# Edge-gated graph layer: the gates' turn ahead of the hot tiles' products, and those products in alternation with the segment sums

## The chip, the cores and the metric

The kernel runs on one core of a Trainium2 chip. A core has five engines with a queue each: PE (matrix products), DVE (vector work), ACT (activations and scaled copies), POOL (here only the issue of indirect gathers) and SP (DMA issue). SBUF holds the working data and PSUM takes what PE writes. The metric is the device time of one execution in microseconds (us), lower is better; the median of several runs counts.

## The reference: what is computed

A graph of 12,500 nodes with 128 features each and 412,500 directed edges, sorted by destination, self loops among them. For each edge the difference of two rows is taken, a gate is computed from it, and the gated differences are summed per destination. The result is added to the input and normalised row by row.

```python
theta = x[dst] - x[src]
w = jax.nn.sigmoid(jax.nn.relu(theta @ W1 + b1) @ W2 + b2)
agg = jax.ops.segment_sum(w * theta, dst, num_segments=n_nodes)
indeg = jax.ops.segment_sum(jnp.ones((dst.shape[0], 1), x.dtype), dst, num_segments=n_nodes)
out = layernorm(x + agg + indeg * (x @ W4 + b4))      # eps 1e-5, no scale or shift
```

All is float32; in this input b1 is scaled by 26.638.

## The kernel before

**Parts.** The edges are worked off in parts. After 18 parts of another kind (`early_part`) come 246 "hot" parts, `part(s)` with s from 18 to 263, and four calls that drain what is open. Two parts make a block of 104 destinations (`WB`); s is even for the first half of a block and odd for the second, which the code keeps as `h`. A hot part is a software pipeline: it turns and gates the hot edges of part t = s + 1, weighs the gathered edges of part s, and brings sums of part s − 1 or s to the block's accumulator `pa`.

**Two kinds of edges.** The sources that are used most are held in SBUF as tables of rows (`tabs`). Edges with such a source, the hot edges, get their rows as a matrix product on PE: a 0/1 tile (`of`, made by DVE) times a table. `hot_products` (L1064 to L1083) issues 24 such bf16 products a part, in four groups of six; three groups go to the PSUM tile `pd`, the fourth to spare columns (from 3P on) of the tile `px`, which the program calls `halves[1]`. `hot_out` copies `pd` into `xT` in SBUF (L1096, ACT), `last_out` copies the spare columns of `px`, by the same line. The other edges are gathered: POOL issues eight indirect DMAs for each part (L405, `gather(s + 3)` from `spread_ahead`), into `zbuf`. The first of the eight carries a wait, `paced[s + 3] = newest[0]`: `newest[0]` is the latest product or sum that the program has issued on PE, so the gathers of a set wait for the end of PE's work in part s − 1.

**One part on PE.** In this order: `hot_turned` (L1135, L1138: the hot differences times W1, into `pz` and `px`); eight products y (L910) for the gathered edges; `hot_rows` (L1152: times W2; L1155: five transposes of `xT`, two into `pz`, three into `px`); the 24 hot products (L1081); `hot_gates_turned` (L1164, L1167: the gates turned into columns of `pz`); last the sums (L1204, in `products`). An odd part's sums are `begin_block`: L1215, L1216 and L828, then eight products of `wx` with the one-hot `ow`. An even part's sums are `add_block`: two records of a carry, 20 products of `wxh` with `owh`, eight of `wx`, thirty records in all. The counts are those of matmul records in the trace.

**One part on ACT.** `hot_out` (L1096 from `pd`), `hot_relu` (L1144, two), in odd parts `total` (L1258, L833), `one_hot` (L885, L886), `hot_gates` (L1159, the sigmoid), in odd parts `shift` (L1198, L1199), `hot_weights` (L1174 copies the turned gates, L1177 copies five tiles scaled by them, two out of `pz` and three out of `px`), `last_out` (L1096 from `px`), in odd parts `own` (L1277, L1279), `gate_sums` (L996, L1000) and `weigh_rest` (L1014, eight scaled copies of gathered rows). Some parts add a square root (L1314) for the normalisation.

**Order.** PE, DVE and ACT take their instructions in the order that the program writes (`tc.manual_schedule(engines=IN_ORDER)`). An engine stops at an instruction whose wait isn't met, and everything behind it waits too. Waits between engines are set by the framework from the tiles that an instruction reads and writes; a tile is one thing for this, so a reader of some columns of `px` waits for the latest writer of `px`. The body of `part(s)` is the order: a call that stands earlier there stands earlier in each of its engines' queues.

Of the kernel before, what the change touches and what calls it, by code (L numbers as in the profile page):

```python
# [25 lines left out]
SUB = 2  # L26
# [60 lines left out]
def gnn_resnorm(  # L87
# [641 lines left out]
    with tc.manual_schedule(engines={SP}), tc.tile_pool(name="work", bufs=2) as wp, tc.tile_pool(  # L729
# [333 lines left out]

        def hot_products(f, x=0, banks=None):  # L1064

            i0, g, i1, i = f
            m = i1 - i0
            of = hot_of(turn_of[0] % 2, x * EP, m * EP).rearrange("p t (m e) -> p t m e", e=RU * HE)
            if not x:
                last = halves[1][:, 3 * P:3 * P + HB * EB] if halves else wide()[:, :HB * EB]  # L1070
                banks = ps_l.tile([P, G, P], F32, name="pd").rearrange("p g e -> p (g e)"), last
            pa, pb = banks[0][:, x * EA:(x + m) * EA], banks[1][:, x * EB:(x + m) * EB]
            for q in range(RG):
                e0, e1 = (0, 2 * HE) if not q else ((q + 1) * HE, (q + 2) * HE)
                if q < RG - 1:
                    to = pa.rearrange("p (m e) -> p m e", e=RG * HE)[:, :, e0:e1]
                else:
                    to = pb.rearrange("p (m e) -> p m e", e=HE)
                for j in range(HT * TERMS):
                    i, t = divmod(j, HT)  # L1080
                    newest[0] = nc.tensor.matmul(to, tabs[:, g, i, q, t, :], of[:, t, :, e0:e1],  # L1081
                                                 start=j == 0, stop=j == HT * TERMS - 1)
            return banks, pa, pb  # L1083
# [117 lines left out]
        def products(to, terms, first, last):  # L1201

            for i, (one, w) in enumerate(terms):
                newest[0] = nc.tensor.matmul(to if len(w.shape) == 3 else to[:, 0, :], one, w,  # L1204
                                             start=first and i == 0, stop=last and i == len(terms) - 1)

# [13 lines left out]
        def add_up(s, halves=(0, 1)):  # L1220
# [8 lines left out]
            if h and b and end:  # L1229
                terms.append((blocks[b]["sh"][:WB, :WB], carry[0][:WB, :AW]))  # L1230
            products(blocks[b]["pa"][:, 1:, :], terms, h == 0 and begin, h == 1 and end)
            if end:
# [8 lines left out]
        def begin_block(b):  # L1241

            sums_of(b)
            products(blocks[b]["pa"], terms_of(b * SUB), True, False)

        def add_block(b):
# [4 lines left out]
            terms += terms_of(b * SUB + 1)  # L1251
            products(d["pa"], terms, False, True)

# [133 lines left out]
        def products_of_tiles():  # L1387

            banks = None
            for f, x in tiled:  # L1390
                banks, pd, last = hot_products(f, x, banks)
                opened.append((f, pd))
                last_of.append((f, last))
            tiled.clear()
            turn_of[0] += 1

# [21 lines left out]
        def early_part(s):  # L1418
# [44 lines left out]
            else:  # L1463
                for t in range(s + 1, s + 2 if s + 1 < PLAIN else s + 3):
                    spread_y(t)
                add_up(s - 1)
            if tiled:
                products_of_tiles()
            if s < PLAIN - 1:
# [80 lines left out]
        def part(s):  # L1550
# [18 lines left out]
            if t < NS:  # L1569
                hot_turned(t)  # L1570
            while opened:
                hot_out(*opened.pop(0))
            if t < NS:
# [9 lines left out]
            if t < NS:  # L1583
                hot_rows(t)
            if tiled:
                products_of_tiles()
            if h == 0 and b + 1 < NK:
                one_hot(b + 1, BP, RW)
            if h == 1 and b + 2 < NK:
                one_hot(b + 2, 0, BP)  # L1590
            if t < NS:
                hot_gates(t)
                hot_gates_turned(t)
            if h == 0 and PLAIN // SUB <= b - 1 < NK:
                add_block(b - 1)
            if h == 1 and b < NK:
                begin_block(b)
            if h == 1 and b < NK:
                shift(b)
            if t < NS:  # L1600
                hot_weights(t)
            last_out()
            if done_b:
# [219 lines left out]
```

## Time and profile before

Three runs of the kernel took 4184.16, 4187.04 and 4194.22 us.

| what | value |
|---|---|
| median of three runs | 4187.04 us |
| profiled execution, its own time | 4190.53 us |
| its span in the profile | 4188.7 us |
| mean granted PE clock | 0.807 |
| PE busy / PE weight loads busy | 76% / 56% of the span |
| DVE / ACT / POOL busy | 55% / 55% / 49% of the span |
| matmul records | 20496 |
| gathers (L405) of the hot parts | 1962 |

How to read the views. A line of the page's groups gives the program's line, engine, operation, the tile written and read with the shape, the count, then busy time and mean ns of one, then how long the engine was idle just before such instructions and what ended most of that. The view of waits gives for each pair of waiter and releaser the total, the number of times and the longest. "Remote" stands where no releaser is found in the profile, "issue" where the engine waited for nothing that the profile shows. A timeline row has the start, the length from the first start to the last end, the engine, the line and the count of neighbouring instructions of the same kind; in brackets, the idle time before and its releaser. Ends of matmuls are modelled. A window's row counts the instructions of each engine within it, with the granted PE clock as a share of full speed.

### The profile page before, as it was taken

The numbers are of one execution on the slowest core, as the hardware profiler recorded it, in microseconds if no ns is written. First come the engines' busy times: TensorE is split into PE (matmuls) and PEld (weight loads), VectorE is DVE, ScalarE is ACT, GpSimd is POOL, SyncE is SP. The second block draws the span as 40 slices with busy tenths as digits, with TensorE's granted clock in tenths as the row PEclk, the third lists the DMA queues.
The fourth block names the chain that finished last, engine by engine and source line by source line (L and its number), as shares of the span: only waits on it lengthen the run. The fifth ranks groups of instructions, "written<-read, shape, count | busy, mean of one in ns | idle before, by whom it ended". The sixth has DMA issues, their size and how long they took to land.

```text
span 4188.7 us, 63869 instructions
## 1 busy us (share of the span) xinstructions
PE 3185.1 (76%) x20496; PEld 2365.9 (56%) x20496; DVE 2297.0 (55%) x4117; ACT 2321.6 (55%) x7325; POOL 2034.1 (49%) x2115
## 2 busy tenths in 40 slices
PE   6666777878777777777786778778777787877777
PEld 5445555655555556555564555556555565655555
DVE  7875566566654666656533566665643434334343
ACT  4444555555555555555554555555555555555555
POOL 4444455454554554545444454555445545454542
PEclk7677788888877888888887788888888888888877
DMA  7343333333343333333333333333333333333331
GB/s 255 93 112 92 95 97 100 93 100 98 95 103 94 95 99 94 101 96 95 99 92 89 89 96 99 95 99 98 95 97 95 100 95 101 97 97 97 98 96 43
DMA packets 280856, 416.17 MB, mean 99 GB/s; under 512 B 66862, under 2 KB 208426, under 8 KB 278974
## 3 DMA queue, kind: packets, MB, share of 16 engines
q0 software_dynamic: 100576, 274.08, 23.3%
q1 hardware_dynamic: 177964, 131.53, 13.3%
q10 hardware_dynamic: 1970, 6.40, 0.5%
q8 instruction: 163, 2.67, 0.3%
q14 instruction: 183, 1.50, 0.1%
HBM read 391.06 MB, written 20.71 MB: 98 GB/s over the span
## 4 chain that ended last, share of the span: by engine, by line
PE 40%; ACT 23%; another core or an unknown queue 23%; DVE 5%; issue 4%; DMA 1%; SPq 0%; DVEq 0%; POOL 0%; ACTq 0%; POOLq 0%
PE pa L1204 15%; PE pd L1081 6%; PE y L910 4%; ACT wxh L1177 4%; ACT wx L1014 3%; PE pz L1152 2%; ACT oh L885 2%; PE pz L1138 2%; ACT hr L1159 2%; ACT oh L886 2%; PE pz L1155 2%; DVE zbuf L968 2%; PE pz L1135 2%; PE px L1135 2%
## 5 line engine op out<-in xcount | busy, mean ns | idle before, releaser
L405 POOL DMA_INDIRECT zbuf<-z,src_i x1962 | 1892.2, 964 | 1928.3 <-ACT xT L1096 654.8
L1135 PE MATMUL pz<-xT,wni 128*128 128x320 f32 x492 | 253.5, 607 | 523.8 <-ACT wxh L1177 516.1
L1014 ACT ACTIVATE wx<-zbuf,wx 128x128 f32<-128x128 f32 x1962 | 600.0, 388 | 0.0
L1081 PEld LDWEIGHTS <-tabs 128*128 128x128 bf16 x6072 | 482.5, 108 | 189.1 <-issue 142.2
L1204 PE MATMUL pa<-wx,ow 128*104 128x260 f32 (+1 forms) x2186 | 533.6, 385 | 22.4 <-issue 21.1
L1174 ACT ACTIVATE wxh<-pz 128x5 f32<-128x5 f32 x246 | 44.0, 179 | 892.8 <-remote 782.3
L1297 DVE TENSOR_TENSOR xw<-xw,a 104x128 f32<-104x128 f32 x132 | 38.5, 291 | 858.3 <-ACT xw L1279 843.9
L1269 DVE TENSOR_TENSOR a<-a,pa 104x130 f32<-104x130 f32 x123 | 35.8, 291 | 810.4 <-ACT xuT L833 752.0
L910 PEld LDWEIGHTS y<-y,oh 64*128 64x128 f32 x2058 | 333.6, 238 | 231.6 <-DVE zbuf L968 165.7
L910 PE MATMUL y<-y,oh 64*128 64x128 f32 x2058 | 368.5, 334 | 101.4 <-DVE zbuf L968 72.9
L1081 PE MATMUL pd<-of,tabs 128*128 128x256 bf16 (+3 forms) x4554 | 441.7, 259 | 0.0
L1135 PEld LDWEIGHTS pz<-xT,wni 128*128 128x128 f32 x492 | 104.5, 242 | 582.3 <-ACT wxh L1177 563.6
L1204 PEld LDWEIGHTS pa<-wx,ow 128*104 128x104 f32 x2186 | 356.9, 179 | 118.4 <-issue 46.7
L1159 ACT ACTIVATE hr<-pz,b_c 128x256 f32<-128x256 f32 x246 | 115.1, 468 | 472.4 <-PE pd L1081 230.6
L1204 PE MATMUL pa<-wxh,owh 128*104 128x130 f32 x2460 | 358.4, 309 | 6.0 <-issue 5.8
L1204 PEld LDWEIGHTS pa<-wxh,owh 128*104 128x104 f32 x2460 | 345.7, 201 | 7.5 <-issue 7.4
L979 DVE TENSOR_REDUCE lg<-zbuf 128x8 f32<-128x1024 f32 (+1 forms) x261 | 315.0, 1207 | 12.9
L973 DVE SCALAR_TENSOR_TENSOR zbuf<-zbuf,fix 128x1024 f32<-128x1024 f32 (+1 forms) x261 | 316.7, 1214 | 8.9
L968 DVE TENSOR_TENSOR zbuf<-y,zbuf 128x1024 f32<-128x1024 f32 x246 | 299.4, 1217 | 4.8 <-issue 2.8
L1138 PE MATMUL pz<-oh,y 64*128 64x320 f32 x492 | 265.6, 630 | 4.3 <-issue 4.3
L1138 PE MATMUL px<-oh,y 64*128 64x320 f32 x492 | 265.5, 630 | 0.0
L1081 PE MATMUL px<-of,tabs 128*128 128x128 bf16 (+3 forms) x1518 | 162.0, 229 | 121.3 <-issue 120.3
(320 smaller groups left out, 5591.2 us busy)
## 6 DMA issues: line engine op xcount, KB each, us to landing
hot_src<-hot_s SPq DMA_DIRECT2D x218, 160.0 KB
zbuf<-z,src_i POOLq DMA_INDIRECT x1962
to_all<-off_d SPq DMA_DIRECT2D x246, 80.0 KB
to_all<-off_d SPq DMA_DIRECT2D x246, 64.0 KB
y<-z SPq DMA_DIRECT2D x504, 28.0 KB
xw<-in_x_dram SPq DMA_DIRECT2D x132, 52.0 KB
out_dram<-o SPq DMA_DIRECT2D x132, 52.0 KB
z<-zbuf SPq DMA_DIRECT2D x6, 1024.0 KB
```

The lines of the kernel that those rows point to most:

```text
L405: ins = nc.gpsimd.indirect_dma_start(out=rows_of(s)[:, k, :], out_offset=None, in_=z if s >= NH else x, in_offset=IndirectOffsetOnAxis(ap= ...
L910: nc.tensor.matmul(y[:, j, :], oh[:, (k0 + j) * P:(k0 + j + 1) * P], rows, start=True, stop=True)
L968: nc.vector.tensor_sub(half, yy.to_broadcast([P, 2, n, D]), half)
L973: nc.vector.scalar_tensor_tensor(h[:, at, :], h[:, at, :], 0.0, w2.to_broadcast([P, n, D]), op0=OP.max, op1=OP.mult)
L979: nc.vector.tensor_reduce(lg[:, at, 0], h[:, at, :], AX.X, OP.add)
L1014: nc.scalar.activation(wx[:, k, :D], rows_of(s)[:, k, D:], AF.Copy, scale=wx[:, k, D:D + 1])
L1081: newest[0] = nc.tensor.matmul(to, tabs[:, g, i, q, t, :], of[:, t, :, e0:e1], start=j == 0, stop=j == HT * TERMS - 1)
L1135: nc.tensor.matmul(to, wneg, xT[:, l * HKL:(l + 1) * HKL], start=True, stop=False)
L1138: nc.tensor.matmul(to, y_of(t)[at], oh[at], start=False, stop=True)
L1159: nc.scalar.activation(parts[t]["hr"][:, :2 * P], pz[:, 2 * P:], AF.Sigmoid, bias=b2_c)
L1177: nc.scalar.activation(wx[:, q, :D], turned_at(q), AF.Copy, scale=wx[:, q, D:D + 1])
L1204: newest[0] = nc.tensor.matmul(to if len(w.shape) == 3 else to[:, 0, :], one, w, start=first and i == 0, stop=last and i == len(terms) - 1)
```

## The change

In `part(s)` the sigmoid and the turn of the gates (`hot_gates`, `hot_gates_turned`) move ahead of the hot products. `hot_out`, which stood ahead of the relu, moves behind the turn of the gates; `last_out`, which stood behind `hot_weights`, moves there as well, and since it now comes ahead of the part's products, it copies out those of the part before. `one_hot` comes behind these copies.

`products` and `hot_products` don't issue their matmuls any more, they return them as lists of functions. A new function `issue(first, second)` runs two such lists in four alternating slices: a quarter of the sums, then six hot products (one group), four times. In an odd part that is two records of sums and six products each time, in an even part six to eight and six (a float32 product has two records). `hot_weights` stands behind `issue`, as it stood behind the sums. The last of these matmuls is now a hot product, and `newest[0]` points to it. The three records L1215, L1216 and L828 of an odd part stay ahead of all of them. The early parts issue their products in one piece, as before. No matmul, copy or DMA is added or removed.

```diff
-        def hot_products(f, x=0, banks=None):
+        def hot_products(f, x, banks, steps_of):
...
-                    newest[0] = nc.tensor.matmul(to, tabs[:, g, i, q, t, :], of[:, t, :, e0:e1],
-                                                 start=j == 0, stop=j == HT * TERMS - 1)
+                    steps_of.append(lambda to=to, i=i, q=q, t=t, j=j, a=of[:, t, :, e0:e1]: nc.tensor.matmul(
+                        to, tabs[:, g, i, q, t, :], a, start=j == 0, stop=j == HT * TERMS - 1))
...
         def products(to, terms, first, last):
 
-            for i, (one, w) in enumerate(terms):
-                newest[0] = nc.tensor.matmul(to if len(w.shape) == 3 else to[:, 0, :], one, w,
-                                             start=first and i == 0, stop=last and i == len(terms) - 1)
+            return [lambda i=i, one=one, w=w: nc.tensor.matmul(
+                to if len(w.shape) == 3 else to[:, 0, :], one, w,
+                start=first and i == 0, stop=last and i == len(terms) - 1) for i, (one, w) in enumerate(terms)]
...
         def products_of_tiles():
 
-            banks = None
+            banks, steps_of = None, []
             for f, x in tiled:
-                banks, pd, last = hot_products(f, x, banks)
+                banks, pd, last = hot_products(f, x, banks, steps_of)
                 opened.append((f, pd))
                 last_of.append((f, last))
+            if tiled:
+                turn_of[0] += 1
             tiled.clear()
-            turn_of[0] += 1
+            return steps_of
+
+        def issue(first, second):
+
+            for i in range(G):
+                for run in (first, second):
+                    for one in run[i * len(run) // G:(i + 1) * len(run) // G]:
+                        newest[0] = one()
...
             if t < NS:
                 hot_turned(t)
-            while opened:
-                hot_out(*opened.pop(0))
             if t < NS:
                 hot_relu(t)
...
             if t < NS:
                 hot_rows(t)
-            if tiled:
-                products_of_tiles()
+            if t < NS:
+                hot_gates(t)
+                hot_gates_turned(t)
+            while opened:
+                hot_out(*opened.pop(0))
+            last_out()
             if h == 0 and b + 1 < NK:
                 one_hot(b + 1, BP, RW)
             if h == 1 and b + 2 < NK:
                 one_hot(b + 2, 0, BP)
-            if t < NS:
-                hot_gates(t)
-                hot_gates_turned(t)
+            sums = []
             if h == 0 and PLAIN // SUB <= b - 1 < NK:
-                add_block(b - 1)
+                sums = add_block(b - 1)
             if h == 1 and b < NK:
-                begin_block(b)
+                sums = begin_block(b)
+            issue(sums, products_of_tiles())
             if h == 1 and b < NK:
                 shift(b)
             if t < NS:
                 hot_weights(t)
-            last_out()
             if done_b:
                 own(b - 1)
```

More of the change, by code (lines that the diff above doesn't have):

```diff
@@ L1230, in add_up @@
                 terms.append((blocks[b]["sh"][:WB, :WB], carry[0][:WB, :AW]))
-            products(blocks[b]["pa"][:, 1:, :], terms, h == 0 and begin, h == 1 and end)
+            issue(products(blocks[b]["pa"][:, 1:, :], terms, h == 0 and begin, h == 1 and end), [])
             if end:
@@ L1243, in begin_block @@
             sums_of(b)
-            products(blocks[b]["pa"], terms_of(b * SUB), True, False)
+            return products(blocks[b]["pa"], terms_of(b * SUB), True, False)
         def add_block(b):
@@ L1251, in add_block @@
             terms += terms_of(b * SUB + 1)
-            products(d["pa"], terms, False, True)
+            return products(d["pa"], terms, False, True)
         def total(b):
@@ L1466, in early_part @@
                 add_up(s - 1)
-            if tiled:
-                products_of_tiles()
+            issue([], products_of_tiles())
             if s < PLAIN - 1:
```

2 lines of the change are left out of this document (removed).

## The prediction

> **What bounds the kernel now.** I read the page first, then the waits, then POOL's timeline, and last PE's and ACT's timelines beside windows cut at POOL's own marks.
>
> ```profile
> span 4188.7 us, 63869 instructions
> PE 3185.1 (76%) x20496; PEld 2365.9 (56%) x20496; DVE 2297.0 (55%) x4117; ACT 2321.6 (55%) x7325; POOL 2034.1 (49%) x2115
> L405 POOL DMA_INDIRECT zbuf<-z,src_i x1962 | 1892.2, 964 | 1928.3 <-ACT xT L1096 654.8
> PE 40%; ACT 23%; another core or an unknown queue 23%; DVE 5%; issue 4%; DMA 1%; SPq 0%; DVEq 0%; POOL 0%; ACTq 0%; POOLq 0%
> ```
>
> No engine is full: PE, the busiest, has 24% of the span idle, and 23% of the chain goes to a releaser that the profile doesn't know. The hot parts take nearly all of the span; one instruction that each part has once gives their pitch.
>
> ```profile
> L1174 ACT ACTIVATE wxh<-pz x246: 178/179/185, 392.0 to 4166.4; 128x5 f32<-128x5 f32 x123
> ```
>
> 246 parts begin within 3774.4 us: 15.4 us a part, 30.8 us for a pair (odd part, then even part), about 122.5 pairs. POOL's timeline shows the pair's beat (start, length, operation, idle time before it).
>
> ```profile
> 1975.07 0.95 POOL L405 DMA_INDIRECT zbuf<-z,src_i  x1 [7.92 <-ACT xT L1096]
> 1983.98 0.95 POOL L405 DMA_INDIRECT zbuf<-z,src_i  x1 [0.30 <-issue]
> 1987.40 0.94 POOL L405 DMA_INDIRECT zbuf<-z,src_i  x1 [2.47 <-ACT wxh L1177]
> ...
> 2005.07 0.95 POOL L405 DMA_INDIRECT zbuf<-z,src_i  x1 [7.94 <-ACT xT L1096]
> 2037.85 0.94 POOL L405 DMA_INDIRECT zbuf<-z,src_i  x1 [10.62 <-issue]
> ```
>
> Each part has a set of eight gathers. The first waits for the last PE instruction of an earlier part; the others follow at 1.25 us. So a pair is set, gap, set, gap, and this one took 30.0 us. What lies in each is in the windows (length, then busy time and instruction count of each engine, granted clock, DMA share, GB/s).
>
> ```profile
> core 0: us, PE busy (x) PEld busy (x) DVE busy (x) ACT busy (x) POOL busy (x), PEclk, DMA share, GB/s
> 1975.07:1986.34 11.27, 7.43 (x67) 5.73 (x65) 5.46 (x10) 3.44 (x9) 7.72 (x8) 1.00 0.35 96
> 1998.55:2005.07 6.52, 6.03 (x40) 4.93 (x39) 4.14 (x5) 5.49 (x21) 0.00 (x0) 1.00 0.35 75
> 2017.50:2028.80 11.30, 8.11 (x52) 5.13 (x53) 9.51 (x18) 6.76 (x21) 7.58 (x8) 0.80 0.44 122
> ```
>
> A set is 11.3 us until its last gather has landed. In the first set, the odd part's, PE got all its work in, and the gap was 1.06 us (1986.34 to 1987.40). In the even part's gap PE still had 40 matmuls, and it was 6.52 us; one pair later it was 9.05 us (2028.80 to 2037.85). With 30.8 us a pair, 22.6 us of sets and 1.1 us of odd gap, the mean even gap is 7.1 us. The sets don't change, so the question is what lies in the two gaps.
>
> What fills them is a wait that ends with the set:
>
> ```profile
> ACT wxh L1174 <- remote: 782.3, 118, 9.5
> ACT hr L1159 <- PE pd L1081: 230.6, 55, 5.0
> ACT hr L1159 <- remote: 198.8, 57, 6.7
> ```
>
> ```profile
> 1976.15 0.44 ACT L1144 ACTIVATE hr<-pz 128x320 f32<-128x320 f32 x1 [1.14 <-PE px L1138]
> 1978.61 0.46 ACT L1159 ACTIVATE hr<-pz,b_c 128x256 f32<-128x256 f32 x1
> 1986.55 0.18 ACT L1174 ACTIVATE wxh<-pz 128x5 f32<-128x5 f32 x1 [6.89 <-remote]
> 1987.28 0.89 ACT L1177 ACTIVATE wxh<-px,wxh 128x128 f32<-128x128 f32 x3
> 1988.82 0.29 ACT L996 ACTIVATE wx<-lg,b_c 128x8 f32<-128x8 f32 x1
> 1989.15 2.45 ACT L1014 ACTIVATE wx<-zbuf,wx 128x128 f32<-128x128 f32 x8
> 2022.01 0.41 ACT L1144 ACTIVATE hr<-pz 128x320 f32<-128x320 f32 x1
> 2022.65 0.91 ACT L885 ACTIVATE oh<-to_all,away,mine 128x640 f32<-128x640 bf16 x1
> 2028.95 0.47 ACT L1159 ACTIVATE hr<-pz,b_c 128x256 f32<-128x256 f32 x1 [4.63 <-remote]
> ```
>
> In the odd part the sigmoid (L1159) gets PE's result at once (1978.61), but the copies of the turned gates (L1174) wait until 1986.55, when the set has landed, though PE's rows have the sums that stand behind that turn at 1980.59. In the even part the sigmoid itself waits until the landing (2028.95); 112 of 123 even parts show that. So while a set is in flight, only PE results up to some point reach ACT. How much was through when the sigmoid's last input (L1155) ended tells the two apart:
>
> ```profile
> 1975.07:1978.26 3.19, 3.19 (x31) 2.44 (x30) 0.89 (x2) 2.08 (x6) 2.58 (x3) 1.00 0.27 65
> 2017.50:2024.08 6.58, 6.27 (x33) 3.69 (x34) 4.96 (x9) 6.52 (x21) 5.05 (x6) 0.68 0.41 101
> ```
>
> After 72 instructions of all engines there was no delay; after 103 there was the full one. That PE results pass freely up to a count between these two is my reading; the mechanism isn't in the trace.
>
> **The change part by part.** PE's rows of the two kinds of part and of a slow even gap:
>
> ```profile
> 1974.14 0.70 PE L1135 MATMUL pz<-xT,wni 128*128 128x320 f32 x2
> 1978.10 1.49 PE L1081 MATMUL pd<-of,tabs 128*128 128x256 bf16 x18
> 1979.42 0.50 PE L1081 MATMUL px<-of,tabs 128*128 128x128 bf16 x6
> 1980.59 1.92 PE L1204 MATMUL pa<-wx,ow 128*104 128x260 f32 x8
> 1987.44 1.39 PE L1135 MATMUL pz<-xT,wni 128*128 128x320 f32 x2 [4.94 <-ACT wxh L1177]
> 1999.42 0.33 PE L1164 MATMUL pz<-wni,hr 128*128 128x128 f32 x1 [0.33 <-ACT hr L1159]
> 1999.85 0.47 PE L1204 MATMUL pa<-a,sh 104*104 104x130 f32 x2
> 2000.16 2.39 PE L1204 MATMUL pa<-wxh,owh 128*104 128x130 f32 x20
> 2002.39 1.92 PE L1204 MATMUL pa<-wx,ow 128*104 128x260 f32 x8
> 2030.13 0.76 PE L1204 MATMUL pa<-a,sh 104*104 104x130 f32 x2
> 2030.68 4.54 PE L1204 MATMUL pa<-wxh,owh 128*104 128x130 f32 x20
> 2035.02 2.06 PE L1204 MATMUL pa<-wx,ow 128*104 128x260 f32 x8
> ```
>
> No instruction of work is added or removed; order changes on PE and ACT alone. SP, DVE and POOL keep their order, and the gathers still wait for the last PE instruction of the part, which is now a product (L1081) and not a sum (L1204).
>
> *A new wait of the copies.* The three copies out of px (L1177, 0.89 us) read the tile into which the last products of the part go (columns beside them). They stand behind those products now, so they wait for PE's last instruction of the part; before, in even parts, they ran beside the 4.5 us of sums (1999.85 to 2004.31). Queued behind them on ACT are L996 with L1000 (0.5 us), the eight L1014 (2.45 us) and the next part's relu (L1144). Odd part's set: the relu starts 0.1 + 0.9 + 0.5 + 2.4 = 3.9 us after the even part's last PE instruction, which is 3.1 us into the set, against 1.1 us (1976.15). L1155 ends near 5.1 instead of 3.2 us. Even part's set: the copies stood at the set's start before, too, and the relu stays near 4.4 us (2022.01 is 4.5 us in), L1155 near 5.8 us.
>
> *Odd gap.* At 5.1 us in, 31 matmuls and 30 loads, 4 gathers, some 5 of DVE and 16 of ACT (2 copies, L996, L1000, 8 L1014, 4 as before) are through: 86, halfway between 72 and 103. I take the odd sigmoid as let through: bounds are no delay and the landing. What PE does ahead in a set (67 matmuls here) then has some 14 ACT and DVE instructions more among it, worth 7 or 8 matmuls; eight sums of 0.24 us or products of 0.08 us are left for the gap: 0.6 to 1.9 us by rows, I take 0.8, and the gap is 1.9 us.
>
> *Even gap.* At 5.8 us in, the count is 103 less 5 or 6 of ACT (copies of pd and one_hot's, which now stand behind the sigmoid, and pz copies) and some 4 of PE: 93 to 97, nearer to 103 than to 72. So I take three of four even parts as late to the landing and one as early. *Late:* sigmoid, turn, 24 products and 30 sums all stand behind the landing; before, the products (1.83 us: 1.49 and 0.5, overlapping) were done ahead. Warm, the gap is 1.3 (to the first sum: 1998.55 to 1999.85) + 4.5 + 1.8 + 0.8 (PE's end to POOL, 2004.31 to 2005.07) = 8.4 us, +1.3 on the mean. But PE is idle from 5.8 us to the landing, 5.5 us; after 4.94 us idle L1135 took 1.39 us against 0.70, and the sums beginning at 2030.13 took 7.0 us, until 2037.1, against 4.5. A cold start of 3.3 us loses about 1.2 us more (9.6 us, +2.5); 6.2 cold us, as in 2028.8 to 2035.0, make it 11.0 (+3.9). I take +2.5, the middle. The Trainium skill, page "TensorE: Matmul & The Clock Gate", section "HAM oscillation — how this bites in real kernels", says that PE gaps over about 3.4 us halve its clock; the 1.39 us row agrees. By that rule each late even part begins cold and 8.4 us is out of reach. *Early:* the sigmoid comes some 2.5 us ahead of the landing, 1.7 us of the mixed work is done by then, and 4.6 + 0.8 = 5.4 us stay, −1.7.
>
> *hot_out, last_out, one_hot behind the sigmoid.* ACT did them while it waited (one_hot's first step, L885, is 0.91 us). Behind a late even sigmoid they run beside 6 us of sums and products and cost nothing; the first product waits for hot_out, but a quarter of the sums goes ahead of it. Without that cover, in an odd part with a late sigmoid, the price is bounded by L885 and its like, 1 us.
>
> *Interleaving.* The same products and sums in another order. Each matmul has its own weight load before as after (20496 of each), so a switch adds no load: nothing, between −0.1 and +0.1 us a part.
>
> **Sum.** Odd +0.8, even 0.75 × 2.5 − 0.25 × 1.7 = +1.45: 2.25 us a pair, × 122.5 = 276 us. The profiled execution took 4190.5 us (its span and 1.8 us around it), so 4466 us; it stands 3.5 us above the median of the runs, 4187.0, so 4463 us is forecast. Its own range, from warm starts (+0.8 + 0.55) to every even part late and cold (+0.8 + 3.9), is 4350 to 4760.
>
> **The rivals.** *Both sigmoids late.* The odd count of 86 lies beyond the limit too. The odd gap is then 1.3 + 1.8 + 1.9 (its eight sums) + 0.8 = 5.8 us or more instead of 1.1; with even parts late, (4.7 + 2.5) × 122.5 = +880: about 5070 us. For it: the limit isn't known closer than 72 to 103. Against: odd sigmoids had no delay at all at 72.
>
> *Faster: the gates get through in both parts.* The place is the even sigmoid. Ready at 5.8 us and let through at once or by 8.5 us, PE mixes sums and products into the set, and the 30 sums no longer stand whole in the gap: −1.7 us by the early case above, −2.4 if PE gets 19 of the 54 done and 35 at 0.11 us with POOL's 0.8 stay, against +0.8, so −0.9 to −1.6 us a pair, 3990 to 4080 us. It decides from where the sigmoid starts 2 us or more ahead of the landing in most even parts. For it: 93 to 97 lies below 103, and no products are queued before the sigmoid. Against: 112 of 123 waits.
>
> *Nothing changes:* the copies' new wait is hidden behind gathers and gains cancel, ±12 us; it asks the two parts of the sum to meet by chance.
>
> *The products themselves held PE's results back,* not a count: ahead of them, the gates pass in both parts, both gaps fall to near 2 us, some −5 us a pair, 3600 us. Against: the even sigmoid waits on L1155, which stands ahead of the products.
>
> **How the numbers follow.** Even late, odd through: 0.47. Both late: 0.17. Faster: 0.27. Same: 0.05. Products the cause: 0.04. The range 4060 to 4760 leaves out the both-late case, half of the large gain and edges. What a measurement here can tell from no change is 0.3%, 13 us: faster 0.30, same 0.05, slower 0.65.
>
> **What would show it.** L1177 from px waiting for PE px L1081, 300 to 700 us in total (new); odd L1144 3 us into its set; even L1159 still starting within 0.3 us of the landing in most parts; L1164 in even parts followed by 54 PE instructions in the gap; odd gaps near 1.9 us. Wrong would be: even sigmoids near 6 us into the set with half of the sums ahead of the landing, or odd sigmoids at the landing.

## The result and the profile after

The changed kernel takes 4686.3 us (median of 4 runs, 4661.8 to 4709.9) where the kernel before took 4185.6 us beside it: a ratio of 1.119, 95% interval 1.113 to 1.126, some 500 us slower. The forecast was slower, 4463 us, 276 us more than before.

The page of the changed kernel, with the lines that answer to those of before:

```profile
span 4674.6 us, 64220 instructions
PE 3342.2 (71%) x20496; PEld 2428.7 (52%) x20496; DVE 2310.6 (49%) x4117; ACT 2330.0 (50%) x7325; POOL 2030.0 (43%) x2115
L405 POOL DMA_INDIRECT zbuf<-z,src_i x1962 | 1887.3, 962 | 2416.5 <-issue 2070.4
L1177 ACT ACTIVATE wxh<-px,wxh 128x128 f32<-128x128 f32 x738 | 217.7, 366 | 969.8 <-PE px L1081 933.3
```

ACT, DVE and POOL do the same work in the same busy time. POOL's gathers stand idle 488 us longer than before (2416.5 against 1928.3), and PE is 157 us busier with the same 20496 matmuls, so it ran slower in places. The new wait is there: the px copies (L1177) wait 933 us in all for the last hot products. The pitch of the parts, from the instruction that each part has once:

```profile
L1174 ACT ACTIVATE wxh<-pz x246: 159/161/181, 392.8 to 4652.8; 128x5 f32<-128x5 f32 x123
```

That is 4260.0 / 245 × 2 = 34.78 us a pair, 3.97 us more than before (3774.4 / 245 × 2 = 30.81); × 122.5 = 486 us, and the span grew by 486. The view of waits has among its largest:

```profile
ACT wxh L1177 <- PE px L1081: 933.3, 225, 6.8
PE pz L1164 <- ACT hr L1159: 620.8, 172, 6.6
ACT hr L1159 <- remote: 603.6, 81, 7.8
ACT L1159 <- remote: 164.4, 28, 6.4
```

The last two are the sigmoid (the second its table load) waiting for a releaser that the profile doesn't know: 109 times, about once for each of the 123 even parts. One pair of sets and the start of the next, on POOL's, ACT's and PE's timelines, show where that falls:

```profile
2010.19 0.95 POOL L405 DMA_INDIRECT zbuf<-z,src_i  x1 [11.52 <-issue]
...
2018.97 0.95 POOL L405 DMA_INDIRECT zbuf<-z,src_i  x1 [0.31 <-issue]
2024.50 0.95 POOL L405 DMA_INDIRECT zbuf<-z,src_i  x1 [4.58 <-issue]
...
2033.41 0.94 POOL L405 DMA_INDIRECT zbuf<-z,src_i  x1 [0.30 <-issue]
2046.83 0.95 POOL L405 DMA_INDIRECT zbuf<-z,src_i  x1 [12.47 <-issue]
```

```profile
2009.46 0.89 ACT L1177 ACTIVATE wxh<-px,wxh 128x128 f32<-128x128 f32 x3 [5.78 <-PE px L1081]
...
2012.93 0.41 ACT L1144 ACTIVATE hr<-pz 128x320 f32<-128x320 f32 x1
...
2015.89 0.47 ACT L1159 ACTIVATE hr<-pz,b_c 128x256 f32<-128x256 f32 x1 [0.51 <-PE px L1155]
...
2023.77 0.89 ACT L1177 ACTIVATE wxh<-px,wxh 128x128 f32<-128x128 f32 x3 [2.10 <-PE px L1081]
...
2027.77 0.41 ACT L1144 ACTIVATE hr<-pz 128x320 f32<-128x320 f32 x1
...
2035.94 0.47 ACT L1159 ACTIVATE hr<-pz,b_c 128x256 f32<-128x256 f32 x1 [7.20 <-remote]
```

```profile
2030.31 0.85 PE L1155 MATMUL px<-wni,xT 128*128 128x128 f32 x3
2036.46 0.48 PE L1164 MATMUL pz<-wni,hr 128*128 128x128 f32 x1 [5.31 <-ACT hr L1159]
...
2037.11 0.76 PE L1203 MATMUL pa<-a,sh 104*104 104x130 f32 x2
...
2039.81 1.94 PE L1203 MATMUL pa<-wxh,owh 128*104 128x130 f32 x8
...
2043.45 0.50 PE L1081 MATMUL pd<-of,tabs 128*128 128x128 bf16 x6
...
2045.57 0.50 PE L1081 MATMUL px<-of,tabs 128*128 128x128 bf16 x6
```

In the odd set (from 2010.19) the sigmoid starts 5.7 us in, and all is well. In the even set (from 2024.50) L1155 has ended by 2031.2, 6.7 us in, but the sigmoid starts only at 2035.94, when the last gather (2033.41) has landed. All sums and products of the part then stand behind it, and the next set starts 10.9 us later. The trace's semaphore records have the signals of L1155's last products for pz and px at 2035.85 and 2035.90, where their rows end at 2030.5 and 2031.2 (ends that are modelled). So what came late is the signal of PE's work, and ACT's sigmoid began right behind it. Of 122 even sigmoids in the trace 111 started over 2 us behind the end of L1155, 110 of these between the landing of the last gather and 1.9 us behind it.

That L1155 is itself so far into the even set comes by way of DVE:

```profile
2024.78 0.40 ACT L1279 ACTIVATE xw<-xw,sw 104x128 f32<-104x128 f32 x1
2025.22 0.29 DVE L1297 TENSOR_TENSOR xw<-xw,a 104x128 f32<-104x128 f32 x1 [8.92 <-ACT xw L1279]
2026.63 1.22 DVE L968 TENSOR_TENSOR zbuf<-y,zbuf 128x1024 f32<-128x1024 f32 x1
2027.91 1.16 PE L910 MATMUL y<-y,oh 64*128 64x128 f32 x8 [1.66 <-issue]
```

`own` (L1277, L1279) stands behind the px copies on ACT, DVE's L1297 waits for L1279, and L968 stands behind L1297 in DVE's order. The eight products y (L910), which overwrite the tile that L968 reads, begin as it ends, and L1152 and L1155 come behind them. The relu (L1144) ends at 2028.5, before y does at 2029.1. This holds beyond the pair: in 120 of 122 even sets y begins within 0.15 us of the end of L968, and L1152 starts 1.4 us behind the relu's end in the median. So the px copies set the even set's start through `own` and DVE more than through the relu.

The windows of that set, of the gap behind it and of two stretches of the gap, with the granted clock ahead of the last two columns:

```profile
core 0: us, PE busy (x) PEld busy (x) DVE busy (x) ACT busy (x) POOL busy (x), PEclk, DMA share, GB/s
2024.50:2035.94 11.44, 4.78 (x29) 2.91 (x29) 10.05 (x15) 4.21 (x17) 7.73 (x8) 0.71 0.49 124
2035.94:2046.83 10.89, 10.20 (x58) 8.48 (x58) 0.00 (x0) 4.21 (x13) 0.00 (x0) 0.68 0.15 45
2036.46:2042.86 6.40, 6.40 (x31) 5.67 (x32) 0.00 (x0) 2.96 (x9) 0.00 (x0) 0.50 0.26 76
2042.86:2046.07 3.21, 3.21 (x28) 2.72 (x27) 0.00 (x0) 0.00 (x0) 0.00 (x0) 1.00 0.00 0
```

PE got 29 matmuls into the set, where the pair shown of before had 52, and did 58 in the gap at a granted clock of 0.68: half speed for the first 6.4 us of its work, then full.

For the comparisons below I worked the same numbers out of each kernel's trace: for about 120 sets of each kind, the mean gap from the landing of the last gather to the first gather of the next set, and within the even set the median start of the relu, end of L1155 and start of the sigmoid, in us from the set's first gather. By how the landing is read from the trace, the gaps are good to some 0.4 us. "Chip" is the number that the results give; for the first two rows they give none. Each ratio is to the kernel before as it ran beside that row's runs.

| kernel | chip | odd gap | even gap | relu | L1155 ends | sigmoid | time, us | ratio to before |
|---|---|---|---|---|---|---|---|---|
| before | | 1.2 | 7.0 | 4.6 | 8.6 | 11.5 | 4186 | 1 |
| changed | | 1.65 | 10.6 | 3.3 | 7.7 | 11.5 | 4686 | 1.119 |
| no alternation (e1) | 14 | 1.0 | 10.3 | 3.2 | 7.6 | 11.5 | 4563 | 1.088 |
| gates behind (e2) | 14 | 1.9 | 6.1 | 5.8 | 9.5 | 13.3 | 4109 | 0.980 |
| weights ahead (e3) | 14 | 1.2 | 5.5 | 0.1 | 2.4 | 3.5 | 4034 | 0.960 |
| weighing behind (e4) | 14 | 3.0 | 10.5 | 1.8 | 6.9 | 11.5 | 4817 | 1.147 |
| changed, again (h1) | 12 | 3.4 | 10.9 | 3.3 | 7.2 | 11.6 | 4887 | 1.158 |
| weighed twice (h2) | 12 | 1.3 | 9.0 | 2.4 | 4.9 | 11.5 | 4461 | 1.057 |
| kept warm (h3) | 12 | 3.5 | 12.6 | 3.3 | 7.2 | 11.7 | 5129 | 1.225 |
| one_hot ahead (h4) | 12 | 1.3 | 8.2 | 0.7 | 3.1 | 10.2 | 4367 | 1.038 |

### The profile page after: what moved, and what is told of

Read it like the earlier page. It is cut to its first block, busy times and chain, and to the rows that moved or that the text cites. A ratio compares the mean times of both kernels' runs of the same rounds, so it can differ in the third digit from the quotient of the medians.

```text
span 4674.6 us, 64220 instructions
## 1 busy us (share of the span) xinstructions
PE 3342.2 (71%) x20496; PEld 2428.7 (52%) x20496; DVE 2310.6 (49%) x4117; ACT 2330.0 (50%) x7325; POOL 2030.0 (43%) x2115
## 3 DMA queue, kind: packets, MB, share of 16 engines
q1 hardware_dynamic: 177964, 131.53, 11.6%
## 4 chain that ended last, share of the span: by engine, by line
PE 46%; ACT 26%; another core or an unknown queue 18%; issue 6%; DVE 3%; DMA 0%; SPq 0%; DVEq 0%; ACTq 0%; POOL 0%; POOLq 0%
PE pa L1203 21%; ACT wx L1014 12%; PE pd L1081 9%; ACT wxh L1177 4%; PE px L1081 2%; PE pz L1152 2%; ACT hr L1144 2%; PE pz L1164 2%; PE px L1155 2%; ACT hr L1159 2%; ACT wx L996 1%; PE pz L1167 1%; PE pz L1155 1%; PE y L910 1%
## 5 line engine op out<-in xcount | busy, mean ns | idle before, releaser
L405 POOL DMA_INDIRECT zbuf<-z,src_i x1962 | 1887.3, 962 | 2416.5 <-issue 2070.4
L1177 ACT ACTIVATE wxh<-px,wxh 128x128 f32<-128x128 f32 x738 | 217.7, 366 | 969.8 <-PE px L1081 933.3
L1081 PEld LDWEIGHTS <-tabs 128*128 128x128 bf16 x6072 | 539.2, 111 | 227.0 <-issue 63.8
L1203 PE MATMUL pa<-wx,ow 128*104 128x260 f32 (+1 forms) x2186 | 639.8, 413 | 5.2 <-issue 5.2
L1014 ACT ACTIVATE wx<-zbuf,wx 128x128 f32<-128x128 f32 x1962 | 600.0, 388 | 0.0
L1164 PE MATMUL pz<-wni,hr 128*128 128x128 f32 x246 | 104.4, 425 | 690.6 <-ACT hr L1159 620.8
L1081 PE MATMUL pd<-of,tabs 128*128 128x256 bf16 (+3 forms) x4554 | 585.3, 277 | 0.0
L910 PE MATMUL y<-y,oh 64*128 64x128 f32 x2058 | 364.8, 332 | 233.4 <-DVE zbuf L968 144.9
L1159 ACT ACTIVATE hr<-pz,b_c 128x256 f32<-128x256 f32 x246 | 116.7, 474 | 812.7 <-remote 603.6
L910 PEld LDWEIGHTS y<-y,oh 64*128 64x128 f32 x2058 | 330.2, 235 | 328.7 <-DVE zbuf L968 183.1
L1203 PE MATMUL pa<-wxh,owh 128*104 128x130 f32 x2460 | 483.2, 354 | 0.0
L1203 PEld LDWEIGHTS pa<-wxh,owh 128*104 128x104 f32 x2460 | 442.6, 242 | 7.3
L1297 DVE TENSOR_TENSOR xw<-xw,a 104x128 f32<-104x128 f32 x132 | 38.4, 291 | 638.6 <-ACT xw L1279 638.6
L968 DVE TENSOR_TENSOR zbuf<-y,zbuf 128x1024 f32<-128x1024 f32 x246 | 299.5, 1218 | 4.9 <-issue 2.8
L1135 PE MATMUL px<-xT,wni 128*128 128x320 f32 x492 | 208.0, 506 | 113.6 <-ACT wxh L1177 113.4
L1152 PE MATMUL pz<-hr,w_c 128*32 128x128 f32 x2460 | 211.1, 338 | 75.9 <-ACT hr L1144 54.1
L885 ACT ACTIVATE oh<-to_all,away,mine 128x640 f32<-128x640 bf16 (+1 forms) x245 | 216.0, 882 | 14.5 <-DMA to_all<-off_d 14.5
```

Of the source, the lines that this page charges most:

```text
L405: ins = nc.gpsimd.indirect_dma_start(out=rows_of(s)[:, k, :], out_offset=None, in_=z if s >= NH else x, in_offset=IndirectOffsetOnAxis(ap= ...
L885: nc.scalar.activation(oh, blocks[b]["to_all"][:, c0:c1], AF.Abs, scale=mine, bias=away)
L910: nc.tensor.matmul(y[:, j, :], oh[:, (k0 + j) * P:(k0 + j + 1) * P], rows, start=True, stop=True)
L968: nc.vector.tensor_sub(half, yy.to_broadcast([P, 2, n, D]), half)
L1014: nc.scalar.activation(wx[:, k, :D], rows_of(s)[:, k, D:], AF.Copy, scale=wx[:, k, D:D + 1])
L1081: steps_of.append(lambda to=to, i=i, q=q, t=t, j=j, a=of[:, t, :, e0:e1]: nc.tensor.matmul(to, tabs[:, g, i, q, t, :], a, start=j == 0, st ...
```

## The experiments

**No alternation.** The changed kernel with all 24 products first, then all sums; the gates stay ahead.

```diff
-            for i in range(G):
-                for run in (first, second):
-                    for one in run[i * len(run) // G:(i + 1) * len(run) // G]:
-                        newest[0] = one()
+            for one in second + first:
+                newest[0] = one()
```

> The changed kernel with the alternation undone: all 24 hot products first, then all sums, the gates still ahead of both. Theory A (the even parts' sigmoid gets its input only when the set of gathers has landed, so products and sums stand whole in the gap behind it, on a cold PE): the even gap stays near 10.5 us, the odd one loses at most 0.4 us because the copies out of px no longer wait for the sums: 4620 to 4700 us. Rival B (the alternation itself, or the wait of the px copies for the part's last product, makes the loss): near the time before, 4190 to 4300 us.

Measured 4562.5 us, ratio 1.088 (1.085 to 1.091). Most of the loss stays without the alternation, so B falls in its first form, the alternation itself. The time lies below A's range, since more was regained than A allowed: the odd gap fell by 0.6 us, the even one by 0.3. B's second form, the wait of the px copies, isn't tested here: the copies no longer wait for the sums, but in the profile they wait for a releaser that it doesn't know, odd copies until about the landing of their set, and the even relu (3.2 us) and L1155 (7.6) are as late as in the changed kernel.

```profile
ACT hr L1159 <- remote: 611.4, 83, 8.8
...
ACT wxh L1177 <- remote: 440.2, 108, 4.6
```

**Gates behind.** The changed kernel with the sigmoid and the turn put back behind products and sums, which stay in alternation.

```diff
             if t < NS:
                 hot_rows(t)
-            if t < NS:
-                hot_gates(t)
-                hot_gates_turned(t)
...
             issue(sums, products_of_tiles())
+            if t < NS:
+                last_sum = newest[0]
+                hot_gates(t)
+                hot_gates_turned(t)
+                newest[0] = last_sum
```

> The changed kernel with the sigmoid and the turn of the gates put back behind products and sums; the alternation, and with it the wait of the px copies for the part's last product, stay. Theory A: nothing that PE has to do in the set waits for the sigmoid any more, PE runs ahead with about 20 of the 54 products and sums while the set is in flight, and the even gap is 4.5 to 7 us: 3950 to 4190 us. Rival B: the alternation and the copies' wait are still there, so 4600 us or more.

Measured 4108.7 us, ratio 0.980 (0.976 to 0.983), in A's range: some 2% under the kernel before, and all of the loss is gone. So the alternation and the copies' wait are no harm by themselves; the loss needs the gates' new place beside them. One pair of it on POOL's timeline:

```profile
2002.19 0.94 POOL L405 DMA_INDIRECT zbuf<-z,src_i  x1 [6.66 <-ACT wxh L1174]
...
2015.16 0.94 POOL L405 DMA_INDIRECT zbuf<-z,src_i  x1 [3.27 <-ACT oh L885]
...
2032.55 0.94 POOL L405 DMA_INDIRECT zbuf<-z,src_i  x1 [7.53 <-ACT wxh L1174]
```

A set takes 11.3 us, so the even gap here is 32.55 − 15.16 − 11.3 = 6.1 us, against 10.9 in the pair shown of the changed kernel.

**Weights ahead.** The changed kernel with `hot_weights` ahead of the alternation, right behind the gates, so that no px copy waits for the part's last product.

```diff
+            if t < NS:
+                hot_weights(t)
             issue(sums, products_of_tiles())
             if h == 1 and b < NK:
                 shift(b)
-            if t < NS:
-                hot_weights(t)
```

> The changed kernel with the weighing of the hot tiles (L1174, L1177) ahead of the alternation, so that the px copies no longer wait for the part's last product. Theory A: the next relu comes up to 1 us earlier, but the even sigmoid is still ready only 6 to 7 us into its set and still waits for the landing: even gap 10 us or more, 4580 to 4690 us. Rival B in the form of the copies' wait: 4190 to 4300 us.

Measured 4033.6 us, ratio 0.960 (0.953 to 0.967). My theory A missed by 550 us: it had said that the even sigmoid would be late all the same. B's form for the copies' wait had the way right, and its range lay 156 us too high. But the trace shows the two as one chain. With the copies free, ACT does the copies, `own`, L996, L1000 and the eight L1014 within the odd set; DVE's L968 ends 1.0 us ahead of the even set (median) instead of 3.4 us into it, the relu comes 0.1 us into the set instead of 3.3, L1155 ends at 2.4 instead of 7.7, and the sigmoid starts at 3.5. Only 37 of 122 even sigmoids are over 2 us late, and the waits for an unknown releaser shrink from 109 to 39:

```profile
ACT hr L1159 <- remote: 194.5, 32, 11.1
...
ACT L1159 <- remote: 36.5, 7, 7.6
```

So the theory was rewritten (A2): what decides is how far into its set the even sigmoid's input is ready, and the new wait of the px copies sets that. A2 took the weighing and the relu, queued behind the copies, for the link between the two; by the rows above it is `own` and DVE.

**Weighing behind.** The changed kernel with the ten weighing instructions of a part moved behind the next part's sigmoid.

```diff
             last_out()
+            while unweighed:
+                gate_sums(unweighed[0])
+                weigh_rest(unweighed.pop(0))
...
-                gate_sums(s)
-                weigh_rest(s)
+                unweighed.append(s)
```

> The changed kernel with the weighing of the gathered rows (L996, L1000, eight L1014: ten ACT instructions, 2.9 us) moved from the end of a part behind the next part's sigmoid. Theory A: the relu starts about 3 us earlier, the even part's L1155 is ready near 3 us into its set with about 75 instructions of all engines through instead of 95, the even sigmoid passes before the landing, half of the products and sums are done within the set, even gap 4 to 6 us: 3900 to 4150 us. Rival C (the even sigmoid waits for the landing whatever its place in the set): even gap stays over 9.5 us, 4550 us or more.

Measured 4817.0 us, ratio 1.147 (1.143 to 1.152): the expectation failed. The even relu did come earlier (1.8 us into the set instead of 3.3), but L1155 ended only 0.8 us earlier, because the y products ahead of it wait for DVE's L968, which ends 3.4 us into the set as in the changed kernel: `own` still stands behind the px copies. The sigmoid stayed late. And the odd sums now wait for L1014, which goes with 1.3 us more of odd gap. A PE row and two waits of this kernel:

```profile
2006.16 1.16 PE L910 MATMUL y<-y,oh 64*128 64x128 f32 x8 [1.66 <-DVE zbuf L968]
```

```profile
ACT hr L1159 <- remote: 738.9, 87, 9.2
...
PE pa L1203 <- ACT wx L1014: 269.2, 124, 3.4
```

It also weakens the count of instructions as the measure: with ten fewer of ACT ahead of it the sigmoid was as late.

**Four more, on a chip that behaves otherwise.** To test A2, the kernel with the weights ahead got the odd part's weighing twice, which delays the even relu. Beside it went the changed kernel with matmuls that should keep PE warm, and two variants of the weights ahead: without alternation, and with `one_hot` back in ACT's wait.

```diff
# weighed twice
-                gate_sums(s)
-                weigh_rest(s)
+                for _ in range(1 + h):
+                    gate_sums(s)
+                    weigh_rest(s)
...
# kept warm
+            while opened:
+                hot_out(*opened.pop(0))
+            last_out()
             if t < NS:
                 hot_gates(t)
+                if h == 0 and tiled:
+                    for _ in range(12):
+                        nc.tensor.matmul(halves[1][:, 3 * P:3 * P + HB * EB], ident,
+                                         xT_all[:, (t - PLAIN) % HX, :HB * EB], start=True, stop=True)
                 hot_gates_turned(t)
-            while opened:
-                hot_out(*opened.pop(0))
-            last_out()
...
# no alternation: issue as in the first experiment
...
# one_hot ahead
+            if h == 0 and b + 1 < NK:
+                one_hot(b + 1, BP, RW)
+            if h == 1 and b + 2 < NK:
+                one_hot(b + 2, 0, BP)
             if t < NS:
                 hot_gates(t)
                 hot_gates_turned(t)
```

> The kernel with the weights ahead of the alternation (4034 us), and in odd parts the weighing of the gathered rows (L996, L1000, eight L1014) done twice in a row with the same result: 2.9 us more of ACT ahead of the relu that opens the even part, and nothing else changed. Theory A2 (what counts is how far into its set the even sigmoid's input is ready; the changed kernel's wait of the px copies matters because it moves the weighing and the relu into the set): the even relu goes from 0.1 to about 3 us into its set, most even sigmoids wait for the landing again, even gap 8 to 10.5 us: 4350 to 4650 us. Rival D (the copies' wait for the part's last product costs by itself, the place of the relu doesn't matter): ACT has 45% idle, so 4034 to 4150 us.

> The changed kernel with twelve more matmuls on PE in each even part, between L1155 and the turn of the gates, whose result is overwritten unused (some 4 us of PE that would be idle), and for their sake hot_out and last_out ahead of the gates again. Theory A: the sigmoid stays late, but PE is warm when the gap begins: even gap 8.4 to 9.3 us instead of 10.6, 4400 to 4540 us. Rival E (a cold clock has no part in it): 4650 us or more.

> The kernel with the weights ahead of the alternation (4034 us), and the alternation undone: all hot products, then all sums. Theory A: PE does the same work ahead in the set in either order, within 40 us of 4034. Rival F (the alternation is what makes that kernel faster than the one before): 4120 to 4250 us.

> The kernel with the weights ahead of the alternation (4034 us), and one_hot (L885, L886) ahead of the sigmoid again, in time that ACT waits. Theory A2: 1.5 us less of ACT between the sigmoid and the end of the weighing, relu and sigmoid as early or earlier in their sets: 3960 to 4034 us. If ACT's tail there isn't what sets the next part's start: unchanged within 20 us.

These four ran on chip 4, and there the kernel before takes 3068.9 us (7 runs, 3065.7 to 3071.5) instead of some 4190. Measured: 3645.1, 4194.8, 3368.2 and 3161.1 us, ratios 1.188, 1.367, 1.098 and 1.031. No expectation in us could hold. The traces say why. In none of the four does a sigmoid wait for an unknown releaser; in the kernel weighed twice all its waits are for L1155 itself, and the even sigmoid starts at 5.7 us with L1155's products for pz ended at 5.6:

```profile
ACT hr L1159 <- PE pz L1155: 221.4, 206, 4.6
```

So in these four traces PE's results are not held while gathers are in flight. All four were still slower than the kernel before. Between the third and the fourth, alternation and `one_hot`'s place both differ, so their shares stay open.

**The changed kernel and the kernel weighed twice, again.**

> The changed kernel once more. The four runs before this one were made on a chip on which the kernel before takes 3069 us instead of 4190 and no sigmoid waits for a set of gathers to land; this run goes to whichever chip comes. If PE's results are held here while gathers are in flight (before near 4190 us), it is 4600 to 4720 us again. If they aren't (before near 3070 us), theory A2 has no late sigmoid to offer; what is left is the chain on ACT and PE (px copies behind the last product, weighing, relu, L1155, sigmoid, products): from the run with the twelve more matmuls, which had an even gap of 8.1 us on that chip, less the 4 us of those matmuls: 3500 to 4000 us, so slower than before there as well.

> The kernel with the weights ahead of the alternation and the weighing of odd parts done twice, as before, for a chip with the hold: theory A2 (the place of the even sigmoid's input in its set) 4350 to 4650 us, even gap 8 to 10.5 us; rival D (the place doesn't matter) 4034 to 4150 us. On a chip without the hold: 3645 us again, within 1%.

They ran on chip 12, with the kernel before at 4211.5 us. The changed kernel took 4886.8 us, ratio 1.158 (1.155 to 1.162), 167 us above the range expected for such a chip: the hold is there, the even gap is 10.9 us, and the odd one 3.4, since 58 of 120 odd sigmoids were over 2 us late as well. The kernel weighed twice took 4460.9 us, ratio 1.057 (1.054 to 1.061), in the range of A2 and out of D's. Of 122 even sigmoids 100 started over 2 us behind L1155, against 37 in the kernel with the weights ahead, and 92 of the sigmoid's waits have an unknown releaser again:

```profile
ACT hr L1159 <- remote: 540.7, 70, 9.5
...
ACT L1159 <- remote: 143.5, 22, 8.0
```

What the doubled weighing makes of this is not shown. The two ratios are from two chips (0.960 on 14, 1.057 on 12). The kernel with the weights ahead was not run on chip 12, and its nearest relative there, without the doubling but with `one_hot` ahead (below), has 1.038 and 102 late even sigmoids. Nor is a held result needed for a loss: on chip 4 the kernel weighed twice took 277 and 484 us more than its two relatives (3645.1 against 3368.2 and 3161.1), with no sigmoid held.

**Kept warm, again.**

> The changed kernel with twelve more matmuls in each even part ahead of the turn of the gates, hot_out and last_out ahead of the gates, as before, for a chip with the hold. Theory A: PE is warm when the even gap begins, so the even gap is 8.4 to 9.3 us instead of 10.6, and the ratio to the kernel before falls from 1.12 to 1.16 to 1.05 to 1.09. Rival E (a cold clock has no part in it, or the twelve only add work): ratio 1.12 or more. On a chip without the hold: 4195 us again, within 1%.

Measured 5128.7 us, ratio 1.225, on chip 12. The ratio lies in E's range, but as a test of the clock the run failed by its design: `last_out` reads `px`, so it waited for L1155 and the landing itself, the twelve products behind it too, and they ran in the gap rather than in the idle time. The rows are of use all the same:

```profile
2014.17 0.34 ACT L1096 ACTIVATE xT<-px 128x64 f32<-128x64 f32 x2 [6.95 <-remote]
```

```profile
core 0: us, PE busy (x) PEld busy (x) DVE busy (x) ACT busy (x) POOL busy (x), PEclk, DMA share, GB/s
2019.23:2025.41 6.18, 6.18 (x56) 5.61 (x56) 0.00 (x0) 0.80 (x3) 0.00 (x0) 1.00 0.12 17
```

Behind the twelve, sums and products of an even part ran at full clock and took 6.2 us. In the changed kernel the same work, from 2037.11 to 2046.07 in the pair shown, took 9.0 us. Against that, the cold start costs 2.8 us of this even gap; in the one before it, from 2001.31 to 2009.43, the same sums and products took 8.1 us, 1.9 more.

**one_hot ahead, again.**

> The kernel with the weights ahead of the alternation and one_hot ahead of the sigmoid, for a chip with the hold, where the one without one_hot's move had a ratio of 0.960. Theory A2: one_hot lies in ACT's wait for the sigmoid, the weighing ends some 1.5 us earlier in both parts, and the even sigmoid's input is as early in its set or earlier: ratio 0.94 to 0.965, even gap at most 5.4 us. If the input comes no earlier because PE's hot products set the end of the part: 0.955 to 0.97. On a chip without the hold: 1.031 again, within 1%.

Measured 4367.5 us, ratio 1.038 (1.035 to 1.041), on chip 12: both expectations failed, and this is no improvement. L1155 ended 3.1 us into the even set, but the median sigmoid waited until 10.2:

```profile
ACT hr L1159 <- remote: 584.4, 93, 8.7
```

The odd sigmoids of the same kernel have L1155 at 3.25 us and started within 2 us of it in 117 of 120 sets. Time into the set alone is therefore not the measure either. Nor did the late ones all wait for the landing: 69 of the 102 started ahead of it. Even sets differ by their DMA: SP issued 3 transfers by then (the median over even sets), none in odd sets. Whether that sets the limit was not tried, and since the kernel without `one_hot`'s move was not run on chip 12, the move and the chip can't be told apart either.

Two versions beat both kernels, "gates behind" (0.980) and "weights ahead": 0.960 of the kernel before and 0.86 of the changed one by the ratios (0.960 / 1.119, the second from a chip that isn't recorded), both on chip 14 alone. What "weights ahead" would do on chip 12 is open; with `one_hot` ahead it did worse there than the kernel before.

## Why the prediction was right, and where its sizes were off

**The direction and the mechanism.** The even sigmoid stays at the landing and the 54 products and sums stand whole behind it on a cold PE: the rows at 2035.94 to 2046.83 show it as forecast. The predicted sights came: px copies waiting for L1081 (933 us, above the 300 to 700 that I gave), the odd relu 2.7 us into its set (median), the even sigmoid at the landing, and 58 matmuls in the gap, the turn and the next part's first among them.

**The odd gap** was put at +0.8 us and measured +0.45; the odd sigmoid passed, as taken. On chip 12 it was 3.4 us, 2.2 more than in the trace of before: there 58 of 120 odd sigmoids were late, which is the rival "both sigmoids late" in part.

**The even gap** is the term that was mis-sized: +1.45 forecast, +3.6 measured (10.6 against 7.0). Both factors were low.

The share: I took three of four even parts as late, since 93 to 97 instructions, with L1155 ended 5.8 us into the set, lay between 72 and 103; 111 of 122 were, and most of the others had their input only near the landing or behind it, so that the early case hardly came. L1155 ended at 7.7 us in the median. The 5.8 was built on one pair, which ended it at 6.6 us where the median of before is 8.6, and on the relu alone. The relu came even earlier than I took it (3.3 against 4.4), but the y products between it and L1155 wait for L968, a DVE step that the prediction doesn't have. That the forecast's way held is in this part luck: the limit wasn't known, and the time that put the sigmoid past it was 1.9 us too early.

The price: I took a late gap of 9.6 us, with a cold start of 3.3 us; the 111 late ones have a mean of 10.6. All 111 began the turn at half clock, and it came up 3.3 to 6.7 us later, 5.0 in the mean (6.4 in the pair shown). By my own two points, 1.2 us lost for 3.3 cold and 2.6 for 6.2, 5.0 us lose some 2.0, which makes 10.4: an estimate, near the measured gap. The Trainium skill, page "TensorE: Matmul & The Clock Gate", section "What's actually happening", gives about 3.4 us of sustained work until the clock is up; here that is about the least, and the most is nearly twice that. With +0.45 and +3.6 the sum is 4.05 × 122.5 = 496 us, close to the loss (486 us of span, 501 of the medians).

**The case for a gain** in the even gap (5.4 us when the sigmoid passes) was sized well: in the kernel with the weights ahead, the 85 even sets whose sigmoid came within 2 us of L1155 have 5.1 us in the mean, the 37 late ones 7.3.

**What I argued wrongly** is the part of the px copies. I wrote that in the even set "the copies stood at the set's start before, too, and the relu stays", and costed them at the odd relu alone. That holds against the kernel before. But the copies are the link that keeps the even sigmoid on the wrong side of the limit: the gates' early turn would have let them, and `own` and the weighing behind them, run in the odd set. One line's place was worth some 14% of the time by the ratios, and the prediction did not see that it was the point on which the change turned.

**The limit** was read as a count of instructions between 72 and 103. Two runs speak against a count of all engines as the whole rule (weighing behind: fewer and still late) and against time alone (one_hot ahead). Nor is earlier always better: on chip 14 the kernel with the weighing behind has L1155 earlier than the one without alternation (6.9 against 7.6 us) and is slower, and on chip 12 as many even sigmoids were late with L1155 at 3.1 us as at 4.9. What the limit is stays open.

## What to carry to other kernels

When a result is needed early, move everything on the way from it to the next stage, not just its maker: here the gates came forward, but the copies that use them were queued behind the last product of a shared PSUM tile, another engine's work was queued behind the copies, and the gain turned into a loss. Two users of different columns of one tile wait for each other as if they shared the data; look for that wait before alternating their work. And where a wait in the profile has no known releaser, time the same kernel on a second chip before building on it.

## What the runs showed of the hardware

The same program took 3069 us on one chip and 4186 to 4213 us on others, with runs within 1% of each other on each. On the slower ones PE's results reached ACT late in many sets of gathers. In the changed kernel, with L1155 ended 7.7 us into the even set, 110 of 111 late sigmoids started at the landing of the last gather or up to 1.9 us behind it, none of the odd ones (L1155 at 4.6) was over 2 us late. With earlier inputs the late ones came off within the set as well: 69 of 102 with `one_hot` ahead, 33 of 37 with the weights ahead. On the fast chip no such wait appears in the four traces. That it is the gathers which hold the results is my reading of these times. The kernel before loses some 980 us in ACT's two waits without a known releaser (782 at L1174, 199 at L1159), and it is 1120 us faster on the fast chip; but its trace there was not taken, so a link isn't shown, nor what makes the chips differ.

The granted clock in the changed kernel's trace is 0.5 or 1.0, and its stretches are, but for the last, whole multiples of 3.41 us: from 2029.20 to 2042.86 it was 0.5 for four such steps. PE began its work at 2036.46, 0.4 us behind the end of the second step, and the clock came up at the end of the fourth. In the even gap before it, work began at 2000.66, 1.2 us ahead of the end of a step (2001.90), and the clock came up at the end of the next, 2005.31. How long a start stays cold goes here with where in a step it falls, 4.7 us in one gap and 6.4 in the other.

A rival stays open for the fast chip: the changed kernel itself was not run there, only with twelve more matmuls in each even part (ratio 1.367).
